# A unit's sum over keys: transposes and a VectorE addition in place of a product with a fold matrix

## The chip, the cores and the metric

The kernel runs on one core of a Trainium2 chip. The metric is the device time of one execution in microseconds; the kernel before takes 3836.37 us (median of three runs, 3836.04 to 3836.43). Times within the profile are from one profiled execution of it, counted from the start of its span.

## What is computed

The reference is one post-norm transformer layer on x of 4096 rows by 256, in fp32:

```python
x = layernorm(x + attention(x))
x = layernorm(x + ffn(x))
```

The attention projects x, quantised per row to integers from -8 to 7, with a weight whose entries are -1, 0 or 1 times a scale per output. One projection serves as q, k and v, for 16 heads of width 16. Queries take the usual layout, but keys and values are a plain reshape of the same numbers, so head h's 4096 keys are 256 rows cut in 16 pieces of 16:

```python
q = proj.reshape(B, N, h, dk).transpose(0, 2, 1, 3)
k = proj.reshape(B, h, N, dk)
v = proj.reshape(B, h, N, dk)
q, k = rotary(q, N), rotary(k, N)
att = einsum('bhnr,bhmr->bhnm', q @ U, k @ U) / sqrt(dk)
y = softmax(att, axis=-1) @ v
return quant4(y) @ ternary_weight(Wo_w).T
```

The feed-forward part has a gated layer (256 to 1024), two hidden layers (1024 to 1024) and one back to 256. What matters here is the end of the attention: the weighted sum over keys, divided by the sum of the weights.

## The kernel before

**Units.** The attention runs as 64 units of work. A unit u is a pair of heads (`pair`, 8 of them) and a block of 512 queries (`qb`, 8 of them), and has 32 steps, one for each 128 keys. Two heads are worked side by side: their keys and queries lie in the upper and lower 64 partitions.

**Three stages, staggered.** A single loop over steps issues everything by hand, in program order, through lists of functions due at a step (`at(step, f)`); there is no scheduler behind it, so each engine works through its instructions in the order of issue.
- `largest` (L472 and L480): two score matmuls with queries on partitions, and two VectorE maxima over 512 keys each, for a unit's row maxima.
- `weights` (L513 and L521): 36 steps later, for the same unit, scores with keys on partitions, less the row maxima (a first matmul with a matrix of -1), then the exponential on ScalarE into `pr`.
- `values` (L535): four steps further, for two steps at a time, eight records on TensorE in the trace. For head j of the pair and k = 0 or 1 (even or odd step), it multiplies the weights with the values and adds to a strip of 32 partitions of the PSUM tile `av`, at partition 32(2j + k). 17 rows of a strip are used: 16 values, and a row of ones that gives the sum of the weights. So a head's sum lies in two strips, one of even and one of odd steps, that still have to be added.

**The order within two steps.** An odd step's list runs first (with `values` in it), then `largest`, then `weights`; an even step has `weights` before `largest`. On TensorE this gives: av group, score pair (L472), weights scores (L513) of two steps, score pair, av group. Two steps take 2.70 us in the middle of a unit.

**The end of a unit.** `finish` has two parts. Part 0 copies `av` to SBUF as `ya` (L550, ScalarE). Part 1, four steps later and ahead of the av group of that step, is what the change touches: it turns `ya` so that queries lie on partitions and adds the even and odd strips, by multiplying each 128 columns of `ya` with `fold` (L556), a matrix of 128 by 34 of zeros and ones; takes the reciprocal of the sums of weights (L564); multiplies (L566); and stores the result to DRAM (L572), from where the feed-forward stage reads it back (L215).

**PSUM banks.** All score pairs of `largest`, the fold product and several transposes share the pool `ps_1` with three banks, taken in turn. A matmul into a bank waits until its last reader is done. The pool `ps_sc` has two tiles for `weights`, `ps_av` one for `av`.

**The fold matrix** is built once at the start, in `set_up`'s function `later`, by two additions on GpSimd from the identity. fp32 transposes with `ident`, of the kind that `nc.tensor.transpose` makes, occur in the key preparation (L365) and in the feed-forward stage (L768, L797).

Of the kernel before, what the change touches and what calls it, by code (L numbers as in the profile page):

```python
# [9 lines left out]
F32 = mybir.dt.float32  # L10
# [4 lines left out]
ALU = mybir.AluOpType  # L15
AX = mybir.AxisListType
PSUM = bass.MemoryType.PSUM

P = 128
# [3 lines left out]
DK = D // H  # L23
# [7 lines left out]
BT = 4  # L31
# [6 lines left out]
def attn_ffn_kernel(  # L38
# [22 lines left out]
    nc = tc.nc  # L61
# [6 lines left out]
    ident = const.tile([P, P], F32, name="ident")  # L68
# [23 lines left out]
    def ternary(w, wabs, neg, bank, sgn, alpha):  # L92


        nc.scalar.activation(wabs, w, AF.Abs)
        ps = bank([P, 512], F32)
        for k in range(2):
            nc.tensor.matmul(
                ps[:, :D], lhsT=ones, rhs=wabs[:, k, :], start=(k == 0), stop=(k == 1)
            )  # L100
        nc.vector.tensor_scalar(alpha, ps[:, :D], 1.0 / D, None, ALU.mult)
        tot = stat.tile([P, 1], F32, name="ttot")
        nc.vector.tensor_reduce(tot, ps[:, :D], AX.X, ALU.add)
        th = stat.tile([P, 1], F32, name="tth")
        nc.vector.tensor_scalar(th, tot, 1.0 / (D * D), 0.05, ALU.mult, ALU.mult)
        nth = stat.tile([P, 1], F32, name="tnth")
        nc.vector.tensor_scalar(nth, th, -1.0, None, ALU.mult)
        nc.vector.tensor_scalar(neg, w, nth, None, ALU.is_le)
        nc.vector.scalar_tensor_tensor(sgn, w, th, neg, ALU.is_ge, ALU.subtract)
# [128 lines left out]
    with ExitStack() as actx:  # L238
        big = actx.enter_context(tc.tile_pool(name="big", bufs=1))
# [9 lines left out]
        sin_k = big.tile([P, 2, H, HALF], F32, name="sin_k")  # L249

        gmat = big.tile([P, P], F32, name="gmat")

        fold = big.tile([P, 2 * (DK + 1)], F32, name="fold")
        minus = big.tile([P, P], F32R, name="minus")

        m_aug = [big.tile([P, BT, P], F32R, name=f"m_aug{i}") for i in range(2)]
# [1 line left out]
        qpool = actx.enter_context(tc.tile_pool(name="qpool", bufs=2))  # L258
# [5 lines left out]
        def bank1(shape, dt):  # L264
            return ps_1.tile(shape, dt, name="ps1")

        def set_up():

            nc.sync.dma_start(out=x_bufs[0], in_=x_t[:, ts(0, BT), :])
            tw = [ppool.tile([P, 2, D], F32, name=f"tw{i}", tag="pr") for i in range(2)]  # L270
            wabs = ppool.tile([P, 2, 2, D], F32, name="tabs", tag="pr")
            neg = ppool.tile([P, 2, 2, D], F32, name="tneg", tag="pr")
            nc.sync.dma_start(out=tw[0], in_=wqkvT.rearrange("(k p) o -> p k o", p=P))
            small = ppool.tile([P, 2 * QB], F32, name="small", tag="pr")
            ut, ut8, mask = small[:32, :DK], small[:32, P : 2 * P], small[:, 2 * P : 3 * P]
            nc.sync.dma_start(out=ut, in_=uT)
            nc.sync.dma_start(out=mask, in_=blockmask)
            tables = ((cos, cos_q, cos_k), (sin, sin_q, sin_k))
            for src, _, tk in tables:
                nc.sync.dma_start(out=tk, in_=src.rearrange("(a p c) f -> p a c f", a=2, p=P))  # L280
            nc.sync.dma_start(out=bias_bc, in_=bqkv.partition_broadcast(P))
            for src, tq, _ in tables:
                nc.sync.dma_start(out=tq, in_=src.rearrange("(t p) f -> p t f", p=P))
            nc.sync.dma_start(out=x_bufs[1], in_=x_t[:, ts(1, BT), :])
            nc.sync.dma_start(out=tw[1], in_=woT.rearrange("(k p) o -> p k o", p=P))

            ternary(tw[0], wabs[:, 0], neg[:, 0], bank1, sgn_qkv, alpha_qkv)
            nc.gpsimd.tensor_copy(
                ut8.rearrange("r (j e) -> r j e", e=DK), ut.unsqueeze(1).broadcast_to([32, 8, DK])
            )  # L290
            psg = bank1([P, 512], F32)
            nc.tensor.matmul(psg[:, :P], lhsT=ut8, rhs=ut8, start=True, stop=True)
            nc.vector.tensor_tensor(gmat, psg[:, :P], mask, ALU.mult)

            def later():

                nc.gpsimd.memset(minus.bitcast(F32), -1.0)
                for i in range(2):
                    nc.gpsimd.memset(m_aug[i].bitcast(F32), 0.0)
                for j in range(2):  # L300
                    nc.gpsimd.tensor_tensor(
                        fold[:, ts(j, DK + 1)],
                        ident[:, 64 * j : 64 * j + DK + 1],
                        ident[:, 64 * j + 32 : 64 * j + 32 + DK + 1],
                        ALU.add,
                    )
                nc.gpsimd.memset(v_chunk[:, :, :, DK : DK + 1], 1.0)
                nc.gpsimd.memset(v_all[:, :, H * (DK + 1) :], 0.0)
                ternary(tw[1], wabs[:, 1], neg[:, 1], bank1, sgn_o, alpha_o)

            return later
# [234 lines left out]
        def finish(u, part, state={}):  # L546
            pair, qb = divmod(u, NQB)
            if part == 0:
                state[u] = qpool.tile([P, QB], F32, name="ya")
                nc.scalar.copy(state[u], avs.pop(u))  # L550
                return
            ya = state.pop(u)
            ps = ps_1.tile([P, 512], F32, name="ps1")
            y = ps[:, : BT * 2 * (DK + 1)].rearrange("p (t j e) -> p t j e", t=BT, j=2)
            for t in range(BT):
                nc.tensor.matmul(  # L556
                    y[:, t].rearrange("p j e -> p (j e)"),
                    lhsT=ya[:, ts(t, P)],
                    rhs=fold,
                    start=True,  # L560
                    stop=True,
                )
            den = stat.tile([P, BT, 2], F32, name="den")
            nc.vector.reciprocal(den, y[:, :, :, DK])  # L564
            yu = stat.tile([P, BT, 2, DK], F32, name="yu")
            nc.vector.tensor_tensor(  # L566
                yu,
                y[:, :, :, :DK],
                den.unsqueeze(3).broadcast_to([P, BT, 2, DK]),
                ALU.mult,  # L570
            )
            nc.sync.dma_start(  # L572
                out=y_dram[qb].rearrange("(t p) d -> p t d", p=P)[
                    :, :, pair * 32 : (pair + 1) * 32
                ],
                in_=yu.rearrange("p t j e -> p t (j e)"),
            )
# [33 lines left out]
        with tc.manual_schedule():  # L611
# [31 lines left out]
            for u in range(NU):  # L643
                pair, qb = divmod(u, NQB)
                if qb == 2 and pair + 1 < H // 2:
                    def start_keys(pair=pair, u=u):
                        kTs[pair + 1] = kpool.tile([P, N], F32R, name="kT")
                        steps = key_steps(pair + 1, kTs[pair + 1])
                        for i, f in enumerate(steps):
                            at(NKT * u + 40 + 6 * i, f)  # L650
                    at(NKT * u + 8, start_keys)

                def start_queries(u=u, pair=pair, qb=qb):
                    qTs[u] = qpool.tile([P, QB], F32R, name="qT", bufs=3)
                    natural, transposed = query_steps(pair, qb, qTs[u])
                    natural()
                    at(NKT * (u - 1) + 26 if u else 0, transposed)

                if u:
                    at(NKT * (u - 1) + (18 if u == 1 else 6), start_queries)  # L660
                else:
                    start_queries()
                at(NKT * (u + 1) + 2, lambda u=u: largest_rows(u))
                base = NKT * u + LAG
                for kt in range(0, NKT, 2):
                    at(base + kt + 1 + AVLAG, lambda s=NKT * u + kt: values(s))
                at(base + NKT + AVLAG - 1, lambda u=u: finish(u, 0))
                at(base + NKT + AVLAG + 3, lambda u=u: finish(u, 1))
# [251 lines left out]
```

## Time and profile before

| what | value |
|---|---|
| median of three runs | 3836.37 us |
| the profiled execution: its own time | 3834.52 us |
| its span | 3832.7 us |
| mean granted TensorE clock | 0.989 of full speed |
| attention with all three stages running | from about 150 to 3105 us |
| VectorE busy in 400 us of it | 347 to 350 us |
| ScalarE busy in 400 us of it | 279 to 280 us |
| interval between the ends of two units, with no other work due | 46.20 us |
| L556: records, mean | 512, 280 ns |
| L564, L566: instructions, mean | 64, 207 ns; 64, 291 ns |

A group of the profile is named by its line, engine and operation, with the tile written, an arrow, and the tiles read. Shapes are partitions by elements. PE is TensorE's matmul and PEld its weight load, DVE is VectorE, ACT ScalarE, POOL GpSimd, SP the engine whose queue issues most DMAs. A timeline row gives the start, the length, the engine, the line and how many instructions are merged in it; in brackets stands the engine's idle time just before and what ended it. The chain that ended last is followed back from the last instruction, at each step to what released it.

### The profile page before, as it was taken

The page shows a single profiled execution, that of the slowest core. Times are in us where ns is not written, and L with a number is a line of the kernel's source. Part 1 is how long each engine was busy: PE and PEld are TensorE (multiplying, and loading weights), DVE is VectorE, ACT ScalarE, POOL GpSimd, SP SyncE. Part 2 cuts the span into 40 slices and gives each one's busy share as a digit, 9 for nine tenths or more (in the row PEclk, how much of TensorE's full clock was granted, in tenths as well). Part 3 has the DMA queues.
Part 4 walks back from the last instruction along what each step waited for, and adds up shares of the span by engine and source line. Part 5 has one row for each costly group of instructions (what it writes and reads, how often), then busy time and mean ns, then how long its engine had stood idle before and what let it go on. Part 6 is the DMA issues. An engine that isn't in the chain of part 4 may idle for free.

```text
span 3832.7 us, 62064 instructions
## 1 busy us (share of the span) xinstructions
PE 3761.0 (98%) x25163; PEld 2147.2 (56%) x25163; DVE 3051.2 (80%) x5276; ACT 2384.1 (62%) x2694; POOL 459.8 (12%) x777
## 2 busy tenths in 40 slices
PE   6999999999999999999999999999999999999998
PEld 3455555555555555555555555555555548888887
DVE  6888888888888888888888888888888845555544
ACT  1666766766766767766767666666777773333333
POOL 3242011001100110111001100110010000000000
PEclk6999999999999999999999999999999999999999
DMA  1000000000000000000000000000010011000100
GB/s 41 7 14 2 8 8 8 8 8 8 8 8 8 8 8 8 8 8 8 8 8 8 8 8 8 8 2 3 24 46 14 8 36 39 17 17 17 34 6 12
DMA packets 69111, 49.36 MB, mean 13 GB/s; under 512 B 43984, under 2 KB 63696, under 8 KB 68816
## 3 DMA queue, kind: packets, MB, share of 16 engines
q1 hardware_dynamic: 64992, 33.78, 3.4%
q0 software_dynamic: 3824, 11.54, 0.9%
q8 instruction: 199, 3.26, 0.4%
q14 instruction: 96, 0.79, 0.1%
HBM read 36.92 MB, written 8.39 MB: 12 GB/s over the span
## 4 chain that ended last, share of the span: by engine, by line
PE 94%; DVE 5%; ACT 1%; issue 0%; POOL 0%; DMA 0%; SPq 0%; ACTq 0%; DVEq 0%
PE av L535 26%; PE sc L513 24%; PE ps L472 21%; PE ps_mm L752 17%; DVE mx L480 3%; PE ps L556 2%; PE ps L500 1%; PE ps L397 1%; PE ps L443 1%; DVE differ L597 0%; PE ps L371 0%; ACT pr L521 0%; PE ps L147 0%; PE ps L365 0%; DVE ma L119 0%
## 5 line engine op out<-in xcount | busy, mean ns | idle before, releaser
L480 DVE TENSOR_REDUCE mx<-ps 128x1 f32<-128x512 f32 x4096 | 2559.9, 684 | 372.3 <-PE ps L472 354.0
L521 ACT ACTIVATE pr<-sc 128x1024 f32<-128x1024 f32 x2048 | 2012.7, 1024 | 915.5 <-PE sc L513 911.3
L472 PEld LDWEIGHTS ps<-kT,qT 64*128 64x128 f32 x4096 | 562.9, 185 | 998.3 <-DVE mx L480 643.2
L472 PE MATMUL ps<-kT,qT 64*128 64x512 f32 x4096 | 1080.6, 470 | 17.9 <-DVE mx L480 14.7
L535 PE MATMUL av<-pr,v_all 128*32 128x512 f32 x8192 | 1092.0, 605 | 0.0
L513 PE MATMUL sc<-mrow,minus 64*128 64x512 f32 x4096 | 866.9, 406 | 3.1 <-ACT pr L521 3.0
L513 PE MATMUL sc<-qT,kT 64*128 64x512 f32 x4096 | 833.5, 391 | 0.0
L513 PEld LDWEIGHTS sc<-qT,kT 64*128 64x128 f32 x4096 | 408.5, 185 | 77.5
L513 PEld LDWEIGHTS sc<-mrow,minus 64*128 64x128 f32 x4096 | 402.4, 185 | 76.1 <-ACT pr L521 18.5
L535 PEld LDWEIGHTS av<-pr,v_all 128*32 128x32 f32 x8192 | 161.6, 108 | 255.7 <-issue 251.9
L785 ACT ACTIVATE gate<-ps_mm,sc_hs 128x512 f32<-128x512 f32 x128 | 88.3, 690 | 312.5 <-PE ps_mm L752 269.4
L734 DVE CAST h<-gate 128x512 fp32r<-128x512 f32 x128 | 54.4, 425 | 223.0 <-ACT gate L785 222.9
L593 POOL CAST wround<-xs 128x1024 fp32r<-128x1024 f32 x22 | 22.9, 1039 | 1406.2 <-DMA xs<-in_h1T 502.2
L736 DVE TENSOR_TENSOR h<-gate,h 128x512 fp32r<-128x512 f32 x192 | 132.4, 689 | 5.1
L752 PE MATMUL ps_mm<-h,h1a 128*128 128x512 f32 x512 | 128.9, 394 | 0.0
L752 PE MATMUL ps_mm<-h,h2a 128*128 128x512 f32 x512 | 127.1, 390 | 0.0
L752 PE MATMUL ps_mm<-h,h2b 128*128 128x512 f32 x512 | 126.5, 389 | 0.0
L752 PE MATMUL ps_mm<-h,h1b 128*128 128x512 f32 x512 | 126.5, 389 | 0.0
L777 DVE SCALAR_TENSOR_TENSOR gate<-ps_mm,sc_s,gate 128x512 f32<-128x512 f32 x64 | 48.1, 751 | 81.9 <-ACT gate L775 58.0
L752 PEld LDWEIGHTS ps_mm<-h,h1b 128*128 128x128 f32 x512 | 96.1, 188 | 20.1
L752 PEld LDWEIGHTS ps_mm<-h,h2b 128*128 128x128 f32 x512 | 96.1, 188 | 20.0
L752 PEld LDWEIGHTS ps_mm<-h,h2a 128*128 128x128 f32 x512 | 95.6, 188 | 19.5
(148 smaller groups left out, 2030.0 us busy)
## 6 DMA issues: line engine op xcount, KB each, us to landing
xs<-in_x SPq DMA_DIRECT2D x16, 512.0 KB, 4.0
y_dram<-yu SPq DMA_DIRECT2D x64, 64.0 KB, 1.8
xs<-in_h1T SPq DMA_DIRECT2D x8, 512.0 KB, 3.9
xs<-in_h2T SPq DMA_DIRECT2D x8, 512.0 KB, 3.8
yb<-y_dram SPq DMA_DIRECT2D x8, 512.0 KB, 5.0
out<-xs SPq DMA_DIRECT2D x8, 512.0 KB, 2.9
h1a<-in_h1T POOLq DMA_DIRECT2D x2, 1024.0 KB, 6.9
h1b<-in_h1T POOLq DMA_DIRECT2D x2, 1024.0 KB, 6.9
```

What stands on the lines that cost most here:

```text
L397: nc.tensor.matmul(ps[:, ts(k, P)], lhsT=flat[:, ts(4 * i + k, P)], rhs=identr, start=True, stop=True,)
L472: nc.tensor.matmul(ps[j], lhsT=qTs[u][rows, ts(qt, P)], rhs=kTs[u // NQB][rows, ts(ck, 512)], start=True, stop=True,)
L480: nc.vector.tensor_reduce(mxs[u][:, qt, j, ck : ck + 1], ps[j], AX.X, ALU.max)
L513: nc.tensor.matmul(ps[:, j, :], lhsT=minus[rows, :] if first else kTs[u // NQB][rows, ts(kt, P)], rhs=mrows[u][rows, :] if first else qTs[ ...
L521: nc.scalar.activation(pr, ps, AF.Exp)
L535: nc.tensor.matmul(avs[u][strip : strip + 32, :], lhsT=v_all[:, 2 * (2 * pair + j) + a, c * (DK + 1) : c * (DK + 1) + 32], rhs=probs[s + k ...
L556: nc.tensor.matmul(y[:, t].rearrange("p j e -> p (j e)"), lhsT=ya[:, ts(t, P)], rhs=fold, start=True, stop=True,)
L734: eng(dst[:, k, 0, :], g)
L736: nc.vector.tensor_tensor(dst[:, k, 1, :], g, dst[:, k, 0, :].bitcast(F32), ALU.subtract)
L752: nc.tensor.matmul(ps, lhsT=sb[:, ks, ts(o, P)] if split else wo[:, k, :], rhs=src[:, k, i, :], start=(k == 0 and i == 0), stop=(k == n - ...
L777: nc.vector.scalar_tensor_tensor(g, pb, scales["s2"][:, o : o + 1], gate, ALU.mult, ALU.mult)
L785: nc.scalar.activation(g, ps, AF.Gelu, scale=scales[sc][:, o : o + 1])
```

## The change

A unit's `ya` is turned by four plain fp32 transposes into a full PSUM bank, in which 128 columns for each block of queries hold four strips of 32. A VectorE reduction then adds even and odd strips straight out of PSUM: it reads 8 groups (block and head) of 17 columns, each as a pair 32 columns apart, and writes the sums to a new SBUF tile `y` of 8 times 17. Reciprocal and product read `y` instead of PSUM. The fold matrix and its two GpSimd additions are gone. All else is issued in the same order as before; on TensorE as many instructions are issued as before, on VectorE 64 more.

```diff
@@ -249,8 +249,6 @@
         gmat = big.tile([P, P], F32, name="gmat")
-
-        fold = big.tile([P, 2 * (DK + 1)], F32, name="fold")
         minus = big.tile([P, P], F32R, name="minus")
@@ -297,13 +295,6 @@
                     nc.gpsimd.memset(m_aug[i].bitcast(F32), 0.0)
-                for j in range(2):
-                    nc.gpsimd.tensor_tensor(
-                        fold[:, ts(j, DK + 1)],
-                        ident[:, 64 * j : 64 * j + DK + 1],
-                        ident[:, 64 * j + 32 : 64 * j + 32 + DK + 1],
-                        ALU.add,
-                    )
                 nc.gpsimd.memset(v_chunk[:, :, :, DK : DK + 1], 1.0)
@@ -551,15 +542,17 @@
             ya = state.pop(u)
             ps = ps_1.tile([P, 512], F32, name="ps1")
-            y = ps[:, : BT * 2 * (DK + 1)].rearrange("p (t j e) -> p t j e", t=BT, j=2)
             for t in range(BT):
-                nc.tensor.matmul(
-                    y[:, t].rearrange("p j e -> p (j e)"),
-                    lhsT=ya[:, ts(t, P)],
-                    rhs=fold,
-                    start=True,
-                    stop=True,
-                )
+                nc.tensor.transpose(ps[:, ts(t, P)], ya[:, ts(t, P)], ident)
+
+            both = ps.rearrange("p (n k e) -> p n k e", k=2, e=32)[:, :, :, : DK + 1]
+            y = qpool.tile([P, BT, 2, DK + 1], F32, name="y")
+            nc.vector.tensor_reduce(
+                y.rearrange("p t j e -> p (t j) e"),
+                both.rearrange("p n k e -> p n e k"),
+                AX.X,
+                ALU.add,
+            )
             den = stat.tile([P, BT, 2], F32, name="den")
             nc.vector.reciprocal(den, y[:, :, :, DK])
```

## The prediction

> **What bounds the kernel now.** I read the page's busy shares first, then the chain that ended last, then the costliest groups, and last the timeline around one unit's end.
>
> ```profile
> PE 3761.0 (98%) x25163; PEld 2147.2 (56%) x25163; DVE 3051.2 (80%) x5276; ACT 2384.1 (62%) x2694; POOL 459.8 (12%) x777
> ...
> PE 94%; DVE 5%; ACT 1%; issue 0%; POOL 0%; DMA 0%; SPq 0%; ACTq 0%; DVEq 0%
> PE av L535 26%; PE sc L513 24%; PE ps L472 21%; PE ps_mm L752 17%; DVE mx L480 3%; PE ps L556 2%; PE ps L500 1%; PE ps L397 1%; PE ps L443 1%; DVE differ L597 0%; PE ps L371 0%; ACT pr L521 0%; PE ps L147 0%; PE ps L365 0%; DVE ma L119 0%
> ```
>
> TensorE leads. The edited product (L556) is 2% of the chain by itself, about 65 us of 3833: whatever TensorE saves there lies on the path. But VectorE, 87% busy in the attention stage (349 to 350 us of each 400 us window), is close behind, and the change hands it work. So the timeline decides:
>
> ```profile
> 2031.74 2.48 DVE L480 TENSOR_REDUCE mx<-ps 128x1 f32<-128x512 f32 x4 [0.21 <-PE ps L472]
> ...
> 2032.47 0.51 PE L472 MATMUL ps<-kT,qT 64*128 64x512 f32 x2
> ...
> 2033.08 1.08 PE L556 MATMUL ps<-fold,ya 128*128 128x34 f32 x8
> ...
> 2034.09 1.07 PE L535 MATMUL av<-pr,v_all 128*32 128x512 f32 x8
> 2034.20 0.21 DVE L564 RECIPROCAL den<-ps 128x8 f32<-128x8 f32 x1
> 2034.44 0.29 DVE L566 TENSOR_TENSOR yu<-ps,den 128x128 f32<-128x128 f32 x1
> ...
> 2035.09 0.19 PEld L472 LDWEIGHTS ps<-kT,qT 64*128 64x128 f32 x2 [0.84 <-DVE yu L566]
> 2035.09 0.50 PE L472 MATMUL ps<-kT,qT 64*128 64x512 f32 x2
> ...
> 2035.62 0.69 DVE L480 TENSOR_REDUCE mx<-ps 128x1 f32<-128x512 f32 x1 [0.89 <-PE ps L472]
> ```
>
> Let T0 be the start of the fold product (2033.08). TensorE: fold to T0+1.01, then the av group to T0+2.01, then the next score pair, whose first maximum can start at T0+2.54. VectorE: its last maximum runs until it starts the reciprocal at T0+1.12, yu ends at T0+1.65, and then it is idle for 0.89 us. I looked at each unit's end: all 62 before the last two have these times within 0.02 us. The "0.84 <-DVE yu" on L472 is not a real wait: the weight load is idle while the av group runs, and yu ended at T0+1.65. In the instruction lists of both programs the next score pair waits for the two preceding maxima, not for the fold's bank (three banks turn), so yu binds nothing there; the pair after it reuses that bank.
>
> Elsewhere a pair of steps takes 2.70 us and is a loop: score pair, first maximum, the score matmul that reuses its bank, av group, score pair. A delay of the first maximum after a unit's end is therefore handed on whole, and so is a gain.
>
> **What the skill says.** "TensorE: Matmul & The Clock Gate", section Terms, gives a TensorE transpose mode that is 4x faster for fp32, and its Part 4 about 275 ns for one transpose in a kernel's context. The trace agrees in kind: an fp32 transpose leaves one record, an fp32 product two.
>
> ```profile
> L556 PE MATMUL ps<-fold,ya 128*128 128x34 f32 x512 | 69.1, 280 | 7.3 <-ACT kT L404 1.2 <-ACT ya L550 0.7
> L371 PE MATMUL ps<-gmat,krT 128*128 128x128 f32 x128 | 18.9, 295 | 0.0
> L365 PE MATMUL ps<-ident,kr 128*128 128x128 f32 x64 | 11.1, 304 | 8.5 <-DVE kr L338 8.5
> L485 DVE TENSOR_REDUCE m<-mx 128x8 f32<-128x64 f32 x64 | 14.1, 221 | 2.2
> L564 DVE RECIPROCAL den<-ps 128x8 f32<-128x8 f32 x64 | 13.3, 207 | 29.7 <-PE ps L556 29.7
> L198 DVE RECIPROCAL rs<-sd 128x4 f32<-128x4 f32 x16 | 2.8, 175 | 10.5 <-ACT sd L194 10.5
> ```
>
> 256 fold products left 512 records; 64 transposes on L365 left 64 (and L797 and L768, also fp32 transposes, 64 for 64). "VectorE: DVE Perf Modes", the perf-mode tier table, has tensor_reduce at one element per cycle from any memory. The trace agrees: (684 - 221 ns) over (512 - 64) elements is 1.03 ns each, with 155 ns fixed, and eight short groups of 8 (L485) cost no more than one long one. "Vector Engine (DVE) Microarchitecture Reference", section 5.2, says that an SBUF stream hopping at every element costs 1.71 to 1.76 ns per column, and 2.50 when two sources, or the output alone, step by 24 words. It says nothing on PSUM, and no row here shows a long read at such a step. The new reduction steps 32 words in its innermost dimension, so this is the unknown of the case.
>
> **The change part by part.**
>
> *TensorE, per unit.* Eight records (four products in two passes) go, from 2033.08 to 2034.09: 1.01 us. Four transposes come. The same four-transpose group on L365 went from 614.83 to 615.41, where the next matmul (L513) started: 0.58. Another such group had its follower, L443, start after 0.41. I take 0.58, as that follower also changes the array's tiling, as av does; 0.41 is kept for the range. Saved: 0.43 us, bounds 0.43 to 0.60. Nothing else in the order moves: the transposes stand where the products stood and wait for the same bank. The next score pair then issues at T0+1.58; its waits are ready (the two maxima end at about T0+0.6 and T0+1.2), and the exponentials that free the sc banks end at about T0+1.13. Its maximum can start at T0+0.58+1.00+0.53 = T0+2.11.
>
> *VectorE, per unit.* One reduction R comes, reading 8 x 17 x 2 = 272 elements, ahead of the reciprocal. It starts where the reciprocal did, T0+1.12, since the transposes are done before (about T0+0.8 by the 0.58 and a drain) and VectorE comes from its last maximum. At the trace's slope R = 155 + 272 x 1.03 = 0.435 us. The reciprocal reads SBUF instead of PSUM: 0.18 (from L198) in place of 0.21. yu keeps 0.29. Each depends on the one before and starts 0.03 after it ends, as den and yu do now. A following independent maximum starts about 0.09 us before the end (L493, 0.18 long, starts at 2018.90, its following maximum at 2018.99), so yu holds the queue 0.20. VectorE is free at T0 + 1.12 + R + 0.03 + 0.18 + 0.03 + 0.20 = T0 + 1.56 + R, that is T0+1.99 at R = 0.435. That is under 2.11: the 0.89 us idle time hides the new reduction. What is queued behind R is den, yu and then the maxima on which the score pairs wait; once R passes 0.55 us every ns of it is on the path. If that cover were gone altogether, it would cost 64 x 0.4 = 26 us.
>
> R's bounds: 0.435 (stride free); 0.62 if a PSUM hop costs the 1.73 of the skill's SBUF row (estimate: 155 + 272 x 1.73 = 626 ns); 0.83 at its 2.50; and at worst what den's row may hide: 207 against 175 ns is 32 more, 4 of it for four more elements, and 28 over 8 elements stepping 17 words in PSUM is 3.5 ns each. On all 272 that gives 0.155 + 272 x 4.53 = 1.39 us. I take 0.435 to 0.55: 28 ns looks more like a fixed cost of a short PSUM read than a per-element one.
>
> *Banks, SP, POOL.* The fold's PSUM bank is freed by R at about T0+1.56, not by yu at 1.65: early enough for its next user after T0+2.8. The store of yu moves to about T0+2.1; it lands 1.8 us after issue, and its readers come units later: nothing. Two POOL additions that built the fold go, in the start-up: 0 taken, at most 0.7 us (two of the 0.33 us of a 128x64 POOL row).
>
> *Sum.* The 62 regular units save 0.43 each. The last two have VectorE idle for 7.7 and 22 us before their reciprocal, so R costs less there and TensorE's part stays. 64 x 0.43 = 27.5 us. The profiled execution took 3834.5 (span 3832.7), so 3807.0; the runs' median is 1.9 above it: 3836.4 - 27.5 = 3808.9.
>
> **The rivals.**
>
> 1. The strided read costs more, and VectorE becomes the bound at unit ends: gain = 2.54 - 1.56 - R. At R = 0.62 it is 0.36 (23 us, 3813.4), at 0.83 0.15 (9.6 us, 3826.8). For it: SBUF's price for hops. Against: the page speaks of SBUF streams only.
> 2. The read costs 4.5 ns per element, as den's row could mean: VectorE is free at T0+2.95, 0.41 after today's start, 64 x 0.41 = 26 us slower, 3862.6. It decides from R = 0.98 us, 3.0 ns per element. For it: the 28 unexplained ns. Against: a fixed cost explains them as well.
> 3. The transposes save TensorE nothing, because fp32 takes two passes there too: as L371's eight records, spaced 0.126, about 0.08 more than the fold per unit: 3841.5. Against: three lines of fp32 transposes with single records.
> 4. The transposes take 0.41: then VectorE's T0+1.99 binds, gain 0.55, 35 us, 3801.2.
>
> **How the numbers follow.** About 0.2% (7.7 us) is what a measurement can tell from no change. TensorE-bound at about 3809, with rival 4 as its low edge: 0.60. Rival 1 with over 7.7 us of gain: 0.24. R so near 0.98 that the change is within 0.2%, or rival 3: 0.06. Rival 2: 0.10. Faster 0.84, same 0.06, slower 0.10. The range reaches from rival 4 (3801) to R = 0.83 (3827) and leaves out about 0.15.
>
> **What would show it.** Right: L556's place holds four records of about 0.27 us, followed by av after 0.58; R is below 0.55 us and starts 1.12 after the first transpose; VectorE's idle time before the next maximum falls from 0.89 to about 0.1 and is still ended by L472; the interval between unit ends falls from 46.20 to 45.77 us. Wrong: R above 0.55, with no idle time before the next maximum and score matmuls waiting for VectorE later in the pair; or two records per transpose; or the chain's VectorE share growing by more than 1%.

## The result, and the profile after

The changed kernel takes 3808.45 us (median of six runs, 3806.62 to 3810.03); the kernel before took 3836.2 us in the six runs beside it. The ratio is 0.9928, with a 95% interval of 0.9915 to 0.9941: 27.8 us faster. The profiled execution took 3807.1 us, with a span of 3805.3. One of the 14 executions of a later kernel, the one with a spare sum (e1), took 8578.12 us and is left out of its median.

The page of the changed kernel: busy time of the engines, and the chain that ended last by line (seven lines of code fewer, so L556 is L546 now, L480 is L471, L535 is L526, and so on).

```profile
PE 3732.7 (98%) x24907; PEld 2112.6 (56%) x24907; DVE 3075.3 (81%) x5340; ACT 2383.2 (63%) x2694; POOL 458.5 (12%) x775
...
PE 93%; DVE 5%; ACT 1%; issue 0%; POOL 0%; DMA 0%; SPq 0%; ACTq 0%; DVEq 0%
PE av L526 26%; PE sc L504 24%; PE ps L463 21%; PE ps_mm L745 17%; DVE mx L471 3%; PE ps L546 1%; PE ps L491 1%; PE ps L388 1%; PE ps L434 1%; DVE differ L590 1%; PE ps L362 0%; ACT pr L512 0%; PE ps L147 0%; PE ps L356 0%; DVE ma L119 0%
```

TensorE is busy for 28.3 us less and VectorE for 24.1 us more, and the time follows TensorE. The edited line is 1% of the chain instead of 2%. The chain's VectorE share is unchanged at 5%, though VectorE does more.

The timeline of the changed kernel around one unit's end, of the same unit as in the prediction:

```profile
2016.61 0.51 PE L463 MATMUL ps<-kT,qT 64*128 64x512 f32 x2
...
2017.22 0.66 PE L546 MATMUL ps<-ident,ya 128*128 128x128 f32 x4
...
2017.81 1.06 PE L526 MATMUL av<-pr,v_all 128*32 128x512 f32 x8
2018.28 0.43 DVE L550 TENSOR_REDUCE y<-ps 128x136 f32<-128x272 f32 x1
2018.75 0.20 DVE L557 RECIPROCAL den<-y 128x8 f32<-128x8 f32 x1
...
2018.80 0.50 PE L463 MATMUL ps<-kT,qT 64*128 64x512 f32 x2
...
2018.99 0.29 DVE L559 TENSOR_TENSOR yu<-y,den 128x128 f32<-128x128 f32 x1
...
2019.34 0.69 DVE L471 TENSOR_REDUCE mx<-ps 128x1 f32<-128x512 f32 x1
```

With T0 the start of the transposes (2017.22): av at T0+0.59, the score pair at T0+1.58, the next maximum at T0+2.12 instead of 2.54. VectorE's work, from the reduction to yu, lies in between. The maximum's row has no idle time in brackets any more: of 0.89 us, 0.06 are left between the recorded end of yu (2019.28) and its start. The row names nothing that it waited for; that TensorE still sets its start shows in the 0.54 us from the score pair to it, where it was 0.53 before (2035.09 to 2035.62). This is the same within 0.05 us at the 62 regular units but for one yu. An interval between units' ends with no other work due fell from 46.20 to 45.77 us. Over all 61 intervals between the ends of the regular units the time fell from 2912.10 to 2887.29 us, 0.41 us for each.

The groups concerned of the changed kernel, by count, busy time and mean:

```profile
L546 PE MATMUL ps<-ident,ya 128*128 128x128 f32 x256 | 42.0, 287 | 7.5 <-ACT kT L395 1.2 <-ACT ya L541 0.7
L550 DVE TENSOR_REDUCE y<-ps 128x136 f32<-128x272 f32 x64 | 27.6, 431 | 27.5 <-PE ps L546 27.5
L557 DVE RECIPROCAL den<-y 128x8 f32<-128x8 f32 x64 | 13.0, 203 | 2.2
```

256 transposes, 256 records: one pass, by which this document means one matmul record (with its weight load) of an instruction; a product left two. The reduction takes 431 ns against the 435 estimated from the slope of contiguous rows, so reading PSUM at a step of 32 words costs nothing beyond its 272 elements. The 27.5 us ahead of it belong to the last two units alone.

### The profile page after: what moved, and what is told of

Read it like the earlier page. It is cut to its first block, busy times and chain, and to the rows that moved or that the text cites. A ratio compares the mean times of both kernels' runs of the same rounds, so it can differ in the third digit from the quotient of the medians.

```text
span 3805.3 us, 61552 instructions
## 1 busy us (share of the span) xinstructions
PE 3732.7 (98%) x24907; PEld 2112.6 (56%) x24907; DVE 3075.3 (81%) x5340; ACT 2383.2 (63%) x2694; POOL 458.5 (12%) x775
## 4 chain that ended last, share of the span: by engine, by line
PE 93%; DVE 5%; ACT 1%; issue 0%; POOL 0%; DMA 0%; SPq 0%; ACTq 0%; DVEq 0%
PE av L526 26%; PE sc L504 24%; PE ps L463 21%; PE ps_mm L745 17%; DVE mx L471 3%; PE ps L546 1%; PE ps L491 1%; PE ps L388 1%; PE ps L434 1%; DVE differ L590 1%; PE ps L362 0%; ACT pr L512 0%; PE ps L147 0%; PE ps L356 0%; DVE ma L119 0%
## 5 line engine op out<-in xcount | busy, mean ns | idle before, releaser
L471 DVE TENSOR_REDUCE mx<-ps 128x1 f32<-128x512 f32 x4096 | 2560.3, 684 | 320.5 <-PE ps L463 296.6
L526 PE MATMUL av<-pr,v_all 128*32 128x512 f32 x8192 | 1091.4, 605 | 0.0
L526 PEld LDWEIGHTS av<-pr,v_all 128*32 128x32 f32 x8192 | 161.6, 108 | 263.7 <-issue 262.6
```

The costliest lines, as they stand in the source:

```text
L471: nc.vector.tensor_reduce(mxs[u][:, qt, j, ck : ck + 1], ps[j], AX.X, ALU.max)
L526: nc.tensor.matmul(avs[u][strip : strip + 32, :], lhsT=v_all[:, 2 * (2 * pair + j) + a, c * (DK + 1) : c * (DK + 1) + 32], rhs=probs[s + k ...
```

## The experiments

The theory: at a unit's end TensorE's group of four lies on the path in full, and VectorE's addition lies in a stretch that TensorE leaves idle. The gain per unit is TensorE's saving, as long as VectorE is done by the time that the next maximum can start. The rivals: VectorE's work eats part of the gain; what was saved is a wait at the bank and not TensorE's time.

Each time is the median, with the difference to the kernel before in the runs beside it, since these lie between 3834.4 and 3836.2 us.

| kernel | us | difference | ratio, 95% interval |
|---|---|---|---|
| changed, first time | 3808.45 | -27.8 | 0.9928, 0.9915 to 0.9941 |
| changed, again (e9) | 3809.76 | -25.5 | 0.9934, 0.9920 to 0.9947 |
| before, with a spare sum (e1) | 3834.14 | -0.4 | 0.9999, 0.9991 to 1.0007 |
| changed, no sum (e2) | 3808.41 | -26.2 | 0.9933, 0.9920 to 0.9946 |
| changed, sum twice (e3) | 3828.93 | -5.7 | 0.9986, 0.9979 to 0.9992 |
| changed, sum three times (e5) | 3859.59 | +25.2 | 1.0064, 1.0047 to 1.0081 |
| changed, turned twice (e7) | 3836.95 | +2.5 | 1.0006, 0.9998 to 1.0015 |
| product in fp32r (e4) | 3805.66 | -28.9 | 0.9924, 0.9911 to 0.9937 |
| changed, on an even step (e6) | 3802.93 | -31.5 | 0.9917, 0.9901 to 0.9934 |
| the same again (e10) | 3802.61 | -32.6 | 0.9916, 0.9902 to 0.9929 |
| before, on an even step (e11) | 3828.37 | -6.9 | 0.9982, 0.9976 to 0.9989 |
| fp32r, on an even step (e8) | 3799.25 | -35.2 | 0.9908, 0.9892 to 0.9925 |

**VectorE's half alone: a spare sum in the kernel before.**

```diff
+            strips = ya.rearrange("p (n k e) -> p n k e", k=2, e=32)[:, :, :, : DK + 1]
+            spare = qpool.tile([P, BT * 2, DK + 1], F32, name="spare")
+            nc.vector.tensor_reduce(
+                spare, strips.rearrange("p n k e -> p n e k"), AX.X, ALU.add
+            )
             den = stat.tile([P, BT, 2], F32, name="den")
```

> The kernel before, with one more VectorE reduction per unit ahead of the reciprocal: it adds the same strips (8 x 17 x 2 elements at the same steps), but from ya in SBUF, and nothing reads the result. The theory (the new reduction hides in 0.89 us of VectorE's idle time at a unit's end): with the fold product kept, VectorE is free again at T0 + 1.56 + its length, 2.0 to 2.4 us for 0.43 to 0.83 us, ahead of the 2.54 at which the next maximum starts, so no change: 3836 us within 4; the idle time before that maximum falls from 0.89 to 0.46 us or less. The rival (VectorE, 87% busy, hands every added instruction on): 64 x 0.46 us or more, 3865 us or more. The instruction's own length also shows what the step of 32 words costs in SBUF: 0.43 us if nothing, 0.62 to 0.83 us at the prices of the skill's SBUF rows.

Measured: no difference. From its timeline:

```profile
2032.23 1.08 PE L556 MATMUL ps<-fold,ya 128*128 128x34 f32 x8
...
2033.29 0.44 DVE L565 TENSOR_REDUCE spare<-ya 128x136 f32<-128x272 f32 x1
...
2034.77 0.69 DVE L480 TENSOR_REDUCE mx<-ps 128x1 f32<-128x512 f32 x1 [0.60 <-PE ps L472]
```

The next maximum starts at T0+2.54 as in the kernel before, with 0.60 us of idle time left of the 0.89. 28 us of added VectorE work cost nothing, so the rival by which a well-filled VectorE hands all its work on falls. The sum from SBUF takes 444 ns, against 431 from PSUM and 435 estimated from contiguous rows: the step of 32 words costs next to nothing there either.

**TensorE's half alone: transposes without the sum.** The odd strips are left out of the result.

```diff
-            both = ps.rearrange("p (n k e) -> p n k e", k=2, e=32)[:, :, :, : DK + 1]
-            y = qpool.tile([P, BT, 2, DK + 1], F32, name="y")
-            nc.vector.tensor_reduce(
-                ...
-            )
+            y = ps.rearrange("p (t j k e) -> p t j k e", j=2, k=2, e=32)[:, :, :, 0, : DK + 1]
```

> The changed kernel without the reduction: reciprocal and product read the even strips straight from PSUM, and the odd strips are left out of the result. The theory (TensorE sets the end; the reduction is hidden): the next maximum still starts at T0 + 2.12, so 3808 us within 4, as with the reduction. The rival (the reduction takes part of TensorE's gain): 64 x up to 0.46 us faster than the changed kernel, down to 3779 us.

Measured: 26.2 us below the kernel before, within the spread of the changed kernel's two measurements (25.5 and 27.8). The next maximum still starts at T0+2.12, now after 0.54 us of idle time:

```profile
2017.07 0.66 PE L546 MATMUL ps<-ident,ya 128*128 128x128 f32 x4
2017.66 1.07 PE L526 MATMUL av<-pr,v_all 128*32 128x512 f32 x8
2018.13 0.20 DVE L550 RECIPROCAL den<-ps 128x8 f32<-128x8 f32 x1
...
2019.19 0.69 DVE L471 TENSOR_REDUCE mx<-ps 128x1 f32<-128x512 f32 x1 [0.54 <-PE ps L463]
```

Over the 61 intervals between the ends of the regular units the profiled execution takes 2887.2 us, against 2887.3 with the sum. So the sum took nothing from the gain.

**Where the cover ends: the sum twice and three times.** The same instruction is issued again right after itself.

> The changed kernel with the reduction issued twice (the second writes the same sums again). The theory: VectorE reaches the product at T0 + 1.76 + 0.46 = 2.22 and is free for the next maximum 0.20 us later, at 2.42, where TensorE would let it start at 2.12: 0.30 us per unit over 62 units, 19 us more than the changed kernel, 3827 us. Rival one (VectorE's idle time in the following pairs takes it up): 3808 us. Rival two (no cover at all): 64 x 0.46 = 29 us more, 3838 us.

> The changed kernel with the reduction issued three times. With two, the next maximum started at T0 + 2.45, straight from VectorE's queue, and the time rose by 20.5 us over the changed kernel. The theory: the cover is used up, so the third costs its whole 0.46 to 0.48 us at each of 62 units, 29 to 30 us more than two: 3858 us, slower than the kernel before. The rival (idle time later in the pairs takes part of a longer delay): 3835 to 3850 us.

With two, the timeline shows the maximum straight behind yu, and the score pair long issued:

```profile
2028.78 0.66 PE L546 MATMUL ps<-ident,ya 128*128 128x128 f32 x4
...
2029.84 0.43 DVE L550 TENSOR_REDUCE y<-ps 128x136 f32<-128x272 f32 x1
2030.30 0.44 DVE L556 TENSOR_REDUCE y<-ps 128x136 f32<-128x272 f32 x1
2030.36 0.50 PE L463 MATMUL ps<-kT,qT 64*128 64x512 f32 x2
...
2031.02 0.29 DVE L565 TENSOR_TENSOR yu<-y,den 128x128 f32<-128x128 f32 x1
...
2031.23 1.88 DVE L471 TENSOR_REDUCE mx<-ps 128x1 f32<-128x512 f32 x3
```

It starts at T0+2.45, 0.33 us later than with one sum: 62 x 0.33 = 20.5 us, and 20 to 22 us were measured against the changed kernel's two measurements. The third sum moves it to T0+2.92. There TensorE stops, in the next pair, for VectorE:

```profile
2004.28 0.50 PE L463 MATMUL ps<-kT,qT 64*128 64x512 f32 x1 [0.42 <-DVE mx L471]
```

It costs 30.8 us more than two (each against the kernel before in the runs beside it: 25.16 + 5.65), 0.48 us for each of 64 units, the whole of the instruction with its start. The first sum is free, the second costs two thirds, the third everything: the cover ends inside the second, and nothing in the pairs that follow takes a delay back. Three sums are slower than the kernel before, with the same fast transposes.

**TensorE's group doubled: turned twice.**

```diff
-            for t in range(BT):
+            for t in [*range(BT), *range(BT)]:
                 nc.tensor.transpose(ps[:, ts(t, P)], ya[:, ts(t, P)], ident)
```

> The changed kernel with the four transposes issued twice into the same bank. The theory: TensorE's group lies on the path in full; four more transposes at 0.10 to 0.13 us each are 0.42 to 0.52 us per unit, 27 to 33 us more than the changed kernel: 3835 to 3841 us. VectorE's reduction then starts with the end of the transposes, at about T0 + 1.1, and stays hidden. The rival (what the change saved isn't TensorE's time but the wait at the bank): 3808 us.

Measured: 2.5 us above the kernel before, 28 to 30 us above the changed one.

```profile
2033.83 1.09 PE L546 MATMUL ps<-ident,ya 128*128 128x128 f32 x8
...
2034.85 1.06 PE L526 MATMUL av<-pr,v_all 128*32 128x512 f32 x8
2034.96 0.44 DVE L550 TENSOR_REDUCE y<-ps 128x136 f32<-128x272 f32 x1
```

The av group follows the first transpose after 1.02 us instead of 0.59. So four more transposes on the path cost 0.44 us (before rounding, 1.023 - 0.586), 28 us in 64 units, which is about what the change saved; the first four with the turn to av cost 0.59. The rival of the bank wait falls: the wait in front of the group is the same in all three kernels (0.61 to 0.62 us from the score pair to the group), and the time follows the records.

**The other way to one pass: the product in fp32r.** In the kernel before, `fold` and `ya` are held as fp32r, which rounds `ya`; no sum on VectorE.

```diff
-        fold = big.tile([P, 2 * (DK + 1)], F32, name="fold")
+        fold = big.tile([P, 2 * (DK + 1)], F32R, name="fold")
-                state[u] = qpool.tile([P, QB], F32, name="ya")
+                state[u] = qpool.tile([P, QB], F32R, name="ya")
```

> The kernel before with ya and the fold matrix held as fp32r, so that the product takes one pass: it rounds ya. TensorE's half of the change alone, with no VectorE work added. The theory: four records instead of eight, the av group follows 0.55 to 0.59 us after the first, the next maximum starts at T0 + 2.08 to 2.12: 3805 to 3809 us. The rival (a transpose is cheap because of its mode, a product of 128 rows by 34 columns isn't in fp32r either): 3836 us.

Measured: 28.9 us below the kernel before.

```profile
2015.15 0.62 PE L556 MATMUL ps<-fold,ya 128*128 128x34 f32 x4
...
2015.70 1.06 PE L535 MATMUL av<-pr,v_all 128*32 128x512 f32 x8
...
2017.24 0.69 DVE L480 TENSOR_REDUCE mx<-ps 128x1 f32<-128x512 f32 x1 [0.51 <-PE ps L472]
```

The group of four records is followed by av after 0.55 us (0.59 with transposes), and the maximum starts at T0+2.09. What the change saves is the second pass of an fp32 product; a transpose is one way to be rid of it, and not cheaper than a product of one pass.

**A better place: the even step.** TensorE waits about 0.17 us at a unit's end for its bank in all kernels so far: its group starts 0.61 us after the score pair (2016.61 to 2017.22), where the av group elsewhere follows after 0.44. One step later, the bank has long been free.

```diff
-                at(base + NKT + AVLAG + 3, lambda u=u: finish(u, 1))
+                at(base + NKT + AVLAG + 4, lambda u=u: finish(u, 1))
```

> The changed kernel with the second part of finish one step later, on an even step: transposes between the weights scores of the two steps, where the bank that they take has long been free, and reduction, reciprocal and product between the two pairs of maxima. The theory: the 0.17 us that TensorE waits for the bank today goes, and 0.58 to 0.68 us are added to a pair as for the key transposes there; VectorE's 0.9 us fit in the idle time that TensorE leaves by about 0.02 us: 0.08 us per unit less, 3803 us. The rival (VectorE's work now stands ahead of the maxima on which the next pair waits): 0.1 us or more per unit slower than the changed kernel, 3815 us or more.

> Single-pass fp32r product with the fold matrix (ya rounded) in place of transposes and reduction, and one step later as in the run before this. The theory: 0.55 us of TensorE without the wait, VectorE's 0.5 us well inside the idle time: 0.08 to 0.1 us per unit less than with fp32r in the old place (3805.7 us): 3800 us. The rival (the place doesn't matter, or the next pair waits for VectorE): 3806 us or more.

> The changed kernel once more, beside the next two on the same chip, since the differences among the variants are a few us. The theory: 27 to 28 us below the kernel before, as measured first (0.9928); the run without the reduction was 26 us below its own kernel before (0.9933).

> The changed kernel with the second part of finish on an even step once more. The theory: 0.08 us per unit, 4 to 6 us, below the changed kernel of the same call. The rival (the first difference lay between the chips): within 1.5 us of it.

> The kernel before, with the fp32 product kept and only the second part of finish one step later. The theory: the place alone saves what the wait at the bank costs, about 0.07 to 0.1 us per unit, 4 to 6 us below the kernel before: 3829 to 3831 us. The rival (the place helps only where TensorE's group is short): 3834 us.

Measured side by side: 25.5 us below the kernel before for the changed kernel, 32.6 on the even step (31.5 the first time), 6.9 for the fp32 product on the even step. The difference by place is 4 to 7 us, with the transposes and with the product alike, so the rival by which VectorE's work then holds up the next pair falls. Three sizes were missed by 1 to 2 us: 27 to 28 us were expected for the changed kernel (25.5 measured), and 4 to 6 for the place (7.1 with the transposes, 6.9 with the product); the changed kernel's own executions lie between 3806.6 and 3810.0 us. In the two profiled executions, whose spans are 3805.1 and 3801.2 us, the difference is 3.9; over the 61 intervals of regular units it is 4.9 (2887.2 to 2882.3 us), 0.08 us for each, as expected. The timeline of the even step (the first of the two runs) shows why, and how little room is left:

```profile
2013.68 0.51 PE L463 MATMUL ps<-kT,qT 64*128 64x512 f32 x2
...
2014.59 0.42 PEld L546 LDWEIGHTS ps<-ident,ya 128*128 128x128 f32 x4 [0.37 <-issue]
...
2015.43 0.43 DVE L550 TENSOR_REDUCE y<-ps 128x136 f32<-128x272 f32 x1
...
2016.34 3.75 DVE L471 TENSOR_REDUCE mx<-ps 128x1 f32<-128x512 f32 x6
...
2017.08 0.50 PE L463 MATMUL ps<-kT,qT 64*128 64x512 f32 x2
```

The weight load before the transposes no longer waits for VectorE's maximum (in the old place the profile has "0.41 <-DVE mx L471"; "issue" is idle time in which the engine waited for nothing that the profile shows). Two steps with a unit's end take 3.40 us from score pair to score pair, against 3.45 in the old place (2015.35 to 2018.80). That is less than the 0.17 us of the wait, because about 0.10 us are lost again: the transposes start 0.33 us after the score matmuls ahead of them (2014.26 to 2014.59), where more score matmuls would follow after 0.23. VectorE works six maxima without a gap after yu: it is full there.

With the fp32r product on the even step the time is 3799.25 us, the lowest of all, at the price of a rounded `ya`. The lowest that still sums in fp32 is the changed kernel on the even step, 3802.6 to 3802.9 us.

## Why the prediction was right, point by point

**What bounds.** TensorE's chain with VectorE close behind, and a loop that hands on every delay of a unit's first maximum. Shown: doubling the transposes and lengthening VectorE's work beyond its cover both come back in full, one by one with the units.

**TensorE: 0.43 us saved.** Shown: av follows after 0.59 us instead of 1.01, so 0.42, and four more transposes cost 0.44. The row of the key transposes, taken because its follower also changes the array's tiling, was the right one. The lower bound of 0.41 us for the group did not come true.

**VectorE: R = 0.435 us, hidden.** R took 0.431. It was worked out from two rows, L480 and L485. Two rows fix a price per element and a fixed cost, and nothing is left over to test whether short groups cost more; that they don't could not be read from them. R itself, with 136 groups of two, is that test, and it holds.

The prediction chose a fixed cost and not a cost per element for the 28 ns that the reciprocal takes beyond L198. R shows that this was right for the sum: at 3.5 ns more per element it would have taken 1.39 us, so rival 2 falls. But the 28 ns are not the price of a short read of PSUM, as was guessed: the reciprocal still takes 203 ns when it reads SBUF, and 194 from PSUM in the run with the spare sum. It steps 17 words in all three, so these rows say nothing on the step. What the 28 ns are stays open.

Rival 1 rested on prices that the prediction took from the Trainium skill, "Vector Engine (DVE) Microarchitecture Reference", section 5.2, and those come from a program that reads two sources. The same section adds that a one-source op, whose read stream alternates between two regions 16 KiB apart at every element and which writes one word per two read, ran at the full read rate. That is the shape of this sum, at a larger step, and the prediction passed over it. The trace agrees with that sentence at 32 words too: 444 ns from SBUF, where the price of 1.73 gave 626, and 431 ns from PSUM, of which the section says nothing.

**One step was off, and harmless.** The sum was said to start at T0+1.12, because VectorE came from its last maximum then. It starts at T0+1.06, and in the run without the sum the reciprocal does too: in the kernel before, the reciprocal had waited 0.06 us for the fold product, too short a wait for the timeline to name it. The reciprocal took 0.20 instead of 0.18, and yu's 0.20 of queue was right (yu starts at 1.77, and with two sums the maximum starts 0.21 after yu). VectorE is free at T0+1.97, where 1.99 was said: the two errors nearly cancel. The margin is narrow, 0.15 us to the T0+2.12 at which TensorE lets the maximum start.

**The sum.** 27.5 us predicted, 25.5 and 27.8 measured. That it is met so closely is in part luck. In an interval with no other work the gain is the 0.43 us forecast, but over all 61 intervals it is 0.41 us, 24.8 us together and 1.4 less than forecast. The interval before the last unit's end makes up for it: it fell by 1.7 us (38.16 to 36.45), where 0.43 was forecast, so that the two profiled spans still differ by 27.4 us. In the run without the sum that interval fell by only 0.3 us (to 37.86). The cause stays open.

**Nothing for POOL, SP and the banks.** Not tried one by one. The first unit's end begins at 160.72 us instead of 160.81, and between 160.1 and 160.8 in the other runs with the same place, with the fold matrix or without: no effect of the two POOL additions can be told apart there.

## What to carry to other kernels

Work moved from the bounding engine to a nearly full one is judged at the place: what counts is the idle time of the second engine at that point of the loop, not its share of the span. Here 0.89 us of idle time covered both the 0.42 us that TensorE became faster and 0.43 us of new work, while the second such instruction cost two thirds and the third all of its length. Before an fp32 product that only moves or adds elements goes on a critical TensorE, count its records: two against one for a transpose or fp32r is what was won here.

## What the runs showed of the hardware that was not expected

- A VectorE reduction over pairs 32 words apart (272 elements in, 136 out) takes 431 ns from PSUM (441 behind eight transposes or behind another sum) and 444 ns from SBUF, against 435 ns estimated from the slope of contiguous rows.
- An independent VectorE instruction starts before the one ahead of it has ended: the spare sum takes 0.44 us and the reciprocal behind it, which reads another tile, started 0.36 us after its start; a sum that writes the same tile as the one before it started 0.46 us after that one's start.
- An fp32 product of 34 columns leaves two records on TensorE, the same product in fp32r one, and an fp32 transpose of 128 columns one. A record more costs about 0.11 us in each case (worked out from 1.01 us for eight records of the product with the turn to av and 0.55 for four; 1.02 and 0.59 for transposes).
